# A four-layer graph network on one core: first group's products plain and by halves, layer 1's gamma and beta folded into its weights, and the last values of layer 3 moved to the end

## The chip, the cores and the metric

The kernel runs on one core of a Trainium2 chip. The time is the device time of one execution in microseconds, taken as the median of the runs. The profile shows one execution, with the engines PE (TensorE matmul), PEld (TensorE's weight loads, which overlap PE), DVE (VectorE), ACT (ScalarE), POOL (GpSimd) and SP (SyncE, which here issues transfers).

## The reference

128 graphs of 64 nodes with 512 features go through four layers. Each layer normalizes, applies a relu, and adds the output of an attention over the graph's adjacency. All data are 32-bit floats. 128 graphs x 64 nodes are 8192 rows.

```python
# layers 0 and 2 (4 heads of 64), adjacency as mask
h = relu(layernorm(x))
q, k, v = h @ Wq, h @ Wk, h @ Wv                    # 512 -> 256
x = x + softmax(mask(q k^T / 8)) v @ Wo + bo        # 256 -> 512

# layer 1 (8 heads of 64), adjacency | eye as mask
h = relu(layernorm(x))
h = layernorm(h) * gamma + beta                     # a second one, inside the layer
q, k, v = split(h @ w_qkv.T)                        # 512 -> 3 x 512
x = x + softmax(mask(q k^T / 8)) v @ w_out.T + b_out

# layer 3 (8 heads of 64)
h = relu(layernorm(x))
m = h @ map_w.T + map_b
n = m / max(norm of each head, 1e-8)
cos_adj = (n n^T > 0.1)                             # and not masked
q, k = m @ q_w.T + q_b, m @ k_w.T + k_b
p = softmax(mask(q k^T / 8)) * keep
adj = cos_adj * p
sem = h @ gcn_map_w.T + gcn_map_b
x = x + relu((adj @ sem @ gcn_W.T) / (adj.sum(-1) + 1))
```

## The kernel before

The rows go through in 16 groups of 512 (`NG = 16`, each four blocks of 128). The program is written as a set of streams; each yields the engine it wants and a rough duration, and an ordering loop (`Order`) fixes, when the program is built, in which order each engine gets its instructions. On the chip each engine then runs its list in order and waits where data are not there yet. A smaller `prio` wins among streams that could start at the same moment.

A projection of 512 x 512 is done by Winograd's form of Strassen's method: seven products of halves rather than eight, with four sums of weight quarters (`sums_of_a`) and four sums of input quarters (`sums_of_b`) made beforehand, mostly on POOL.

```python
r_qk = ring("qk", 3, [P, NC, TB * P])       # q, k of a group
r_t  = bank("t", 3, [P, NC, 2, H])          # sums of the input quarters
r_v  = bank("v", 2, [P, TB, 8 * (N + 1)])
r_e  = ring("e", 2, [P, 16, N])             # softmax of half a group
r_pt = ring("pt", 1, [P, 2, 4, P])
r_sc = ring("sc", 1, [P, 2, 512], space=ps) # scores and values in PSUM

def product(bank, A, B, tokens_out, first):          # four calls of 128x256
    for m in range(2):
        for k in range(KC):                          # KC = 2 here
            nc.tensor.matmul(...)

def weights():
    for key, parts in units:         # qk0, vo0, q1, k1, v1, o1, qk2, ...
        ...                          # DMA of the parts, from ACT's queue
        w_ready[key].set()
        yield from sums_of_a(o_part(t) if key in ("vo0", "vo2") else t)
        w_sums[key].set()

def scaled_chunks(s, h):             # layer 1 only
    for half in range(2):
        yield n_ready[1, s, half]
    for c in range(NC):
        ...                          # four transposes into pt
        nc.scalar.activation(h[:, c, :], pt..., AF.Identity,
                             bias=beta[:, c:c + 1], scale=gamma[:, c:c + 1])

def transposes(steps):
    for l, s in steps:
        ...
        if l == 1:
            yield from scaled_chunks(s, h)
        for half in range(2 if l != 1 else 0):
            yield n_ready[l, s, half]
            ...                      # four transposes and one copy a block
            nc.scalar.copy(h[:, :, b * P:(b + 1) * P], pt)
        T, t_done[l, s] = yield from r_t.new("T")
        h_ready[l, s].set()
        yield from sums_of_b(quarters(h), T)

class Out:
    def first(self, i, k, p_, read, done):           # the eviction of a product
        if self.bias is None:
            nc.scalar.copy(o, p3)
        else:
            for m in range(2):
                nc.scalar.activation(o[:, m], p3[:, m], AF.Identity, bias=...)
```

In layer 3 a group's projections are `map`, then `sem`, `q`, `k`; in the last group `q`, `k`, `sem`. The values of `sem` get a row added on POOL (`add_rows`, four instructions), and `p_ready` waits for that. A group's softmax comes in two halves (`front`), each followed by the cosine mask, and `last` transposes each half and multiplies it by the values.

```python
order = ("q", "k", "sem") if end else ("sem", "q", "k")
...
def front(l, s):
    for u, blocks in enumerate(units):               # two halves in layer 3
        S, se = yield from scores(z["q"], z["k"], 2 * nch, blocks)
        E, e = yield from softmax_parts(S, se, m, ...)   # E from r_e
        ...
        C, ce = yield from scores(z["n"], z["n"], 4, blocks)
        ...                                          # Cf = C > 0.1, E *= Cf

def last(s):
    for u in range(2):
        yield z["e_ready", u]
        pt, pte = yield from transposed(*z["e", u])
        for b, t in enumerate(blocks):
            po, poe = yield from r_sc.new("po3")
            ...                                      # 32 small products
            od.spawn(finish(s, t, po, poe, got), 0)
```

Of the kernel before, what the change touches and what calls it, by code (L numbers as in the profile page):

```python
# [8 lines left out]
F32 = mybir.dt.float32  # L9
# [194 lines left out]
def gnn_stack(ctx: ExitStack, tc: tile.TileContext, a: dict, out: bass.AP):  # L204
# [65 lines left out]
    vecs = const.tile([P, 6, NC], F32, name="vecs")  # L270
    nc.scalar.dma_start(vecs, a["vecs"].rearrange("p (v c) -> p v c", c=NC))
    gamma, beta, map_b, q_b, k_b, gcn_b = (vecs[:, i, :] for i in range(6))
    gcn_row = const.tile([P, D], F32, name="gcn_row")


# [13 lines left out]
    def o_part(t):  # L289

        return t.rearrange("p a k n -> p (a k) n")[:, 4:11, None, :]
# [24 lines left out]
    def sums_of_b(B, T, vector=False):  # L316

        n = T.shape[2]
        for o, i0, i1 in ((T[:, 0], B(0, 1), B(0, 0)), (T[:, 1], B(1, 1), T[:, 0]),
# [4 lines left out]
            else:  # L324
                yield pool(0.65 * n)
                nc.gpsimd.tensor_tensor(o, i0, i1, ALU.subtract)  # L326

    def weights():
        for key, parts in units:
            if key == "q1":  # L330
                yield p_ready[0, 0]
            t, w_done[key] = yield from r_w.new(f"w_{key}")
            W[key] = t
            for src, dst in parts(t):
                yield ("actq", 1.0, 10.0)
                nc.scalar.dma_start(dst, src.rearrange("(c p) o -> p c o", p=P))
            if key in ("vo0", "o1", "vo2"):
                l = int(key[-1])
                src = a[f"bo{l}"]
                bo[l], bo_done[l] = yield from r_u.new(f"bo{l}")  # L340
                yield ("actq", 0.5, 2.0)
                nc.scalar.dma_start(bo[l], bass.AP(tensor=src.tensor, offset=src.offset,
                                                   ap=[[0, P], [1, D]]))
            if key == "sem3":
                yield from gcn_fold(t)
            w_ready[key].set()
            yield from sums_of_a(o_part(t) if key in ("vo0", "vo2") else t)
            w_sums[key].set()

    def quarter(t, c, i):  # L350

        return t[:, 2 * i + c // 2, c % 2, :]

    def gcn_fold(t):

# [51 lines left out]
                                 scale=rs[:, 0, t:t + 1])  # L407

    hT, hB, h_ready, h_done, t_done = {}, {}, {}, {}, {}

    def quarters(v):

# [29 lines left out]
                normed[l, s, half] = x, xe  # L442
                n_ready[l, s, half].set()

    def scaled_chunks(s, h):

        for half in range(2):
            yield n_ready[1, s, half]
        x = [normed.pop((1, s, half)) for half in range(2)]
        for c in range(NC):  # L450
            pt, pe_ = yield from r_tr.new("ptr")
            for b in range(TB):
                yield pe(0.115)
                nc.tensor.transpose(pt[:, b, :], x[b // 2][0][:, b % 2, c * P:(c + 1) * P], ident)  # L454
            if c == NC - 1:
                for _, xe in x:
                    xe.set()
            yield act(0.6)
            nc.scalar.activation(h[:, c, :], pt.rearrange("p b k -> p (b k)"), AF.Identity,  # L459
                                 bias=beta[:, c:c + 1], scale=gamma[:, c:c + 1])  # L460
            pe_.set()

    def transposes(steps):

        for l, s in steps:
            h, h_done[l, s] = yield from r_h.new("hT")
            hT[l, s] = h
            if l == 1:
                yield from scaled_chunks(s, h)
            for half in range(2 if l != 1 else 0):  # L470
                yield n_ready[l, s, half]
                x, xe = normed.pop((l, s, half))
                for t in range(2):
                    pt, pe_ = yield from r_tr.new("ptr")
                    for c in range(NC):
                        yield pe(0.115)
                        nc.tensor.transpose(pt[:, c, :], x[:, t, c * P:(c + 1) * P], ident)  # L477
                    if t == 1:
                        xe.set()
                    yield act(0.6)  # L480
                    b = 2 * half + t
                    nc.scalar.copy(h[:, :, b * P:(b + 1) * P], pt)  # L482
                    pe_.set()
            if (l, s) == (3, 1):
                yield x_done[2, NG - 1]
            T, t_done[l, s] = yield from r_t.new("T")
            sums = od.event()
            hB[l, s] = (quarters(h), T, sums)
            h_ready[l, s].set()
            yield from sums_of_b(quarters(h), T)  # L490
            sums.set()
# [67 lines left out]
    def winograd(A, BT, tokens_out, out_, used, begun):  # L559
# [46 lines left out]
        od.spawn(out_.alone(1, 0, p_, pe_), 0)  # L606
        od.spawn(when([c11, c12, c22, pe_], used), 0)

    class Heads(Out):


# [50 lines left out]

    st, p_ready, s_ready, p_used, with_ones = {}, {}, {}, {}, []

    def projections(steps):
        for l, s in steps:
            yield h_ready[l, s]
            h, BT = hT[l, s], hB[l, s]
            z = st[l, s] = {}
            end = s == NG - 1  # L670
            if l in (0, 2):
                yield w_ready[f"qk{l}"]
                qk, z["qk_done"] = yield from r_qk.new("qk")
                used = yield from unit(W[f"qk{l}"], (*BT, w_sums[f"qk{l}"]), False, Out(quarters(qk)))
                od.spawn(when([used], s_ready[l, s], t_done[l, s],
                              w_done[f"qk{l}"] if end else None), 0)
                z["q"], z["k"] = qk[:, 0:2, :], qk[:, 2:4, :]
                yield w_ready[f"vo{l}"]
# [7 lines left out]
                od.spawn(when(es, p_ready[l, s], h_done[l, s]), 0)  # L686
            elif l == 1:
                es = []
                for n in "qk":
                    yield w_ready[f"{n}1"]  # L690
                    o, z[f"{n}_done"] = yield from r_qk.new(f"{n}T")
                    es.append((yield from unit(W[f"{n}1"], (*BT, w_sums[f"{n}1"]), False,
                                               Out(quarters(o)))))
                    od.spawn(when([es[-1]], w_done[f"{n}1"] if end else None), 0)
                    z[n] = o
                od.spawn(when(es[:2], s_ready[l, s]), 0)
# [9 lines left out]
            else:  # L706
# [4 lines left out]
                m_sums, z["n_ready"], m_used = od.event(), od.event(), od.event()  # L711
                od.spawn(sums_after(m_ready, mv, z, m_sums), 1)
                od.spawn(norms(mT, s, m_ready, z["n_ready"], m_used), 3)
                order = ("q", "k", "sem") if end else ("sem", "q", "k")
                es, rows = [], od.event()
                for n in order:
                    yield w_ready[f"{n}3"]
                    if n == "sem":
                        V, z["v_done"] = yield from r_v.new("S2")
                        S2 = V.rearrange("p t (h e) -> p t h e", e=N + 1)  # L720
                        if not any(V is v for v in with_ones):

                            with_ones.append(V)
                            yield pool(0.6)
                            nc.gpsimd.memset(S2[:, :, :, N:N + 1], 1.0)

                        def sv(i, k, S2=S2):
                            return S2[:, 2 * k:2 * k + 2, 4 * i:4 * i + 4, 0:N]
                        used = yield from unit(W["sem3"], (*BT, w_sums["sem3"]), True, Heads(sv))
                        od.spawn(when([m_ready, used], t_done[l, s], h_done[l, s]), 0)  # L730
                        od.spawn(add_rows(S2, used, rows), 0)
                        z["v"] = S2
                        continue
                    yield m_sums
                    o, z[f"{n}_done"] = yield from r_qk.new(f"{n}T3")
                    es.append((yield from unit(
                        W[f"{n}3"], (mv, z["T"], w_sums[f"{n}3"]), False,
                        Out(quarters(o), q_b if n == "q" else k_b))))
                    z[n] = o
                    if n == "k":  # L740
                        z["n"] = mT
                        od.spawn(when(es, s_ready[l, s], m_used, z["T_done"]), 0)
                od.spawn(when(es + [rows], p_ready[l, s]), 0)

    def sums_after(e, B, z, done):
        yield e
# [78 lines left out]
                                             lT[r, c, k], rT[r, c, k], start=True, stop=True)  # L825
        return S, e

    def softmax_parts(S, se, mask, neg):

        m = mask.rearrange("p b k -> p (b k)")  # L830
        n = m.shape[1]
# [6 lines left out]
        mx = small.tile([P, 16], F32, tag="mx", name="mx")  # L838
        yield dve(1.2)
        nc.vector.tensor_reduce(mx, S3, AX.X, ALU.max)  # L840
        E, e = yield from r_e.new("E")
        yield dve(1.2)
        nc.vector.tensor_tensor(E, S3, mx[:, :, None].to_broadcast([P, 16, N]), ALU.subtract)  # L843
        se.set()
# [6 lines left out]
        nc.vector.reciprocal(sm, sm)  # L851
        yield pool(1.95)
        nc.gpsimd.tensor_mul(E, E, sm[:, :, None].to_broadcast([P, 16, N]))  # L853
        return E, e

    def transposed(E, e):

# [197 lines left out]
    def front(l, s):  # L1055
# [6 lines left out]
            z["e_ready", u] = od.event()  # L1062
        p_used[l, s].set()
        for u, blocks in enumerate(units):
            S, se = yield from scores(z["q"], z["k"], 2 * nch, blocks)
            if u == len(units) - 1:
                for n in ("q", "k", "qk"):
                    if f"{n}_done" in z:
                        z[f"{n}_done"].set()
            m = mask[:, blocks[0]:blocks[0] + len(blocks)]  # L1070
            E, e = yield from softmax_parts(S, se, m, (0, 1, 0, 2)[l])
            if u == len(units) - 1:
                me.set()
            z["e", u] = E, e
# [22 lines left out]
    def last(s):  # L1097
# [3 lines left out]
        for u in range(2):  # L1101
            blocks = [2 * u, 2 * u + 1]
            yield z["e_ready", u]
            pt, pte = yield from transposed(*z["e", u])
            for b, t in enumerate(blocks):

                po, poe = yield from r_sc.new("po3")
# [24 lines left out]
    def attentions(steps):  # L1132
        for l, s in steps:
            yield p_used[l, s]
            yield p_ready[l, s]
            yield from (attention(l, s) if l < 3 else last(s))


# [61 lines left out]
```

## Time and profile before

| | |
|---|---|
| time, median of 3 runs | 2985.18 us (2980.7 to 2989.06) |
| span of the profiled execution | 2978.9 us |
| POOL's sums of a weight quarter, 128x512 | 1.3 us each |
| matmul calls of a projection by seven products | 28, of 128x256 each |
| ACT, eviction with scale and bias in layer 1's transposes, x64 | 783 ns |
| ACT, eviction of transposes by a copy, x192 | 592 ns |
| ACT, eviction of q in layer 1 by copies, from mA, x48 | 585 ns |
| ACT, eviction of q in layer 3 with a bias, from mA, x96 | 470 ns |

The profile gives the busy time of each engine; a busy PE is a PE with a matmul in flight, which is not a PE at its peak. A row of the timeline has the start in us, the duration in us, the engine, the line of the kernel, the operation, what is written from what, the shapes and the count; in square brackets stands the idle time before it and what ended it. A full-precision matmul leaves two records, so a count of records is twice a count of calls; a transpose leaves one.

### The profile page before, as it was taken

To read this page: it belongs to the slowest core of one execution; us is meant where nothing else is said; L and a number is where in the kernel's file an instruction comes from. 1 tells how busy PE (TensorE), PEld (TensorE's weight loads), DVE (VectorE), ACT (ScalarE), POOL (GpSimd) and SP (SyncE) were. 2 spreads that over 40 slices of the span, in tenths; PEclk is the share of its full clock that TensorE was granted. 3 is DMA by queue.
4 is the path that set the end of the run, shared out by engine and by line. 5 is a ranking of instruction groups with operands and counts; after the bars stand their busy time and mean duration, and the time that the engine had idled before them with its cause. 6 is when DMAs were issued, how large, how long until landed. Compare 5 with 4: busy or idle time off the path is not lost.

```text
span 2978.9 us, 63888 instructions
## 1 busy us (share of the span) xinstructions
PE 2910.6 (98%) x27176; PEld 2468.1 (83%) x27176; DVE 1727.3 (58%) x2748; ACT 1336.6 (45%) x2361; POOL 1465.2 (49%) x1144
## 2 busy tenths in 40 slices
PE   8999999999999999999999999999999999999997
PEld 6888888888888888888888888887888787888876
DVE  5665566664554555445456556556666666665566
ACT  4444445544444444433444444454444444444442
POOL 6666667444344334335566566663344343344332
PEclk9999999999999999999999999999999999999998
DMA  5323333211112112113233332422232222222212
GB/s 163 116 88 123 95 101 126 67 62 66 48 45 73 59 44 73 59 44 98 94 114 104 102 116 88 138 82 64 72 90 83 63 62 66 70 85 71 52 48 62
DMA packets 162957, 244.05 MB, mean 82 GB/s; under 512 B 17392, under 2 KB 69616, under 8 KB 162672
## 3 DMA queue, kind: packets, MB, share of 16 engines
q1 hardware_dynamic: 149760, 226.56, 24.3%
q10 hardware_dynamic: 12912, 13.42, 1.4%
q8 instruction: 213, 3.49, 0.5%
q14 instruction: 72, 0.59, 0.1%
HBM read 168.60 MB, written 71.30 MB: 81 GB/s over the span
## 4 chain that ended last, share of the span: by engine, by line
PE 85%; DVE 6%; ACT 4%; DMA 2%; POOL 2%; issue 1%; SPq 0%; DVEq 0%; ACTq 0%; POOLq 0%
PE mA L516 37%; PE mC L516 18%; PE mB L516 10%; PE sc L824 4%; PE mmv L659 4%; PE ptp L864 3%; PE ptr L477 3%; PE po L983 2%; ACT E L846 1%; PE po L1118 1%; DVE E L843 1%; DVE sc L835 1%; DVE mx L840 1%; PE mmn L773 1%; PE ptr L454 1%
## 5 line engine op out<-in xcount | busy, mean ns | idle before, releaser
L853 POOL TENSOR_TENSOR E<-E,sm 128x1024 f32<-128x1024 f32 x96 | 186.3, 1941 | 424.2 <-DVE sm L851 298.7
L390 DVE BATCH_NORM_STATS2 st<-xin 128x6 f32<-128x512 f32 x320 | 215.6, 674 | 260.2 <-DMA xin<-x 206.9
L929 POOL TENSOR_TENSOR xres<-xres,u 128x512 f32<-128x512 f32 x192 | 243.4, 1268 | 250.0 <-ACT u L924 245.0
L908 POOL TENSOR_TENSOR xres<-xres,u 128x512 f32<-128x512 f32 x192 | 257.7, 1365 | 219.5 <-DMA xres<-x 99.6
L406 ACT ACTIVATE xin<-xin,rs 128x512 f32<-128x512 f32 x320 | 243.7, 808 | 110.9 <-DVE rs L399 110.7
L397 POOL TENSOR_TENSOR rs<-rs,mhalf 128x2 f32<-128x2 f32 x160 | 118.4, 740 | 276.9 <-DVE rs L395 270.3
L659 PE MATMUL mmv<-w_vo,hT 128*128 128x256 f32 x1024 | 233.4, 380 | 0.9 <-DVE xres L542 0.9
L659 PEld LDWEIGHTS mmv<-w_vo,hT 128*128 128x128 f32 x1024 | 193.5, 190 | 29.0 <-DVE xres L542 2.6
L326 POOL TENSOR_TENSOR t<-hT 128x512 f32<-128x512 f32 x128 | 178.3, 1393 | 73.2 <-ACT hT L482 39.0
L326 POOL TENSOR_TENSOR t<-hT,t 128x512 f32<-128x512 f32 x128 | 172.3, 1346 | 50.5 <-ACT hT L459 46.6
L399 DVE SCALAR_TENSOR_TENSOR rs<-mv,rs 128x2 f32<-128x2 f32 x160 | 80.3, 502 | 197.7 <-POOL rs L397 197.7
L516 PE MATMUL mA<-t,w_qk 128*128 128x256 f32 x768 | 187.0, 380 | 2.8 <-ACT qk L529 2.5
L516 PE MATMUL mA<-t,w_k 128*128 128x256 f32 x768 | 182.7, 381 | 4.8 <-ACT kT L533 4.7
L516 PE MATMUL mA<-t,w_q 128*128 128x256 f32 x768 | 187.1, 379 | 0.0
L516 PEld LDWEIGHTS mA<-t,w_k 128*128 128x128 f32 x768 | 144.8, 190 | 28.2 <-ACT kT L533 8.3
L516 PEld LDWEIGHTS mA<-t,w_qk 128*128 128x128 f32 x768 | 143.1, 190 | 22.0 <-ACT qk L529 3.3
L868 ACT COPY pt<-ptp 128x512 f32<-128x512 f32 x192 | 112.7, 588 | 105.1 <-PE ptp L864 105.1
L516 PEld LDWEIGHTS mA<-t,w_q 128*128 128x128 f32 x768 | 143.1, 190 | 18.1
L849 DVE TENSOR_REDUCE sm<-E 128x16 f32<-128x1024 f32 x96 | 116.4, 1212 | 69.5 <-ACT E L846 69.5
L757 POOL TENSOR_TENSOR v<-v,gcn_row 128x512 f32<-128x512 f32 x64 | 81.4, 1305 | 150.4 <-ACT v L615 150.4
L482 ACT COPY hT<-ptr 128x512 f32<-128x512 f32 x192 | 113.7, 592 | 74.1 <-PE ptr L477 74.1
L846 ACT ACTIVATE E<-E 128x1024 f32<-128x1024 f32 x96 | 101.5, 1058 | 83.6 <-DVE E L843 83.3
(210 smaller groups left out, 6819.0 us busy)
## 6 DMA issues: line engine op xcount, KB each, us to landing
x<-xres SPq DMA_DIRECT2D x96, 512.0 KB, 3.8
xin<-x SPq DMA_DIRECT2D x96, 512.0 KB, 3.8
xres<-x SPq DMA_DIRECT2D x64, 512.0 KB, 4.2
xin<-in_x SPq DMA_DIRECT2D x32, 512.0 KB, 3.8
xres<-in_x SPq DMA_DIRECT2D x32, 512.0 KB, 4.6
u<-rs SPq DMA_DIRECT2D x128, 128.0 KB, 3.1
xres<-x SPq DMA_DIRECT2D x256, 64.0 KB, 2.3
out<-xres SPq DMA_DIRECT2D x256, 64.0 KB, 2.1
```

The lines of the kernel that those rows point to most:

```text
L326: nc.gpsimd.tensor_tensor(o, i0, i1, ALU.subtract)
L390: nc.vector.bn_stats(st, v[:, t, :])
L397: nc.gpsimd.tensor_tensor(rs[:, 0, :], rs[:, 1, :], mhalf[:, :2], ALU.pow)
L406: nc.scalar.activation(v[:, t, :], v[:, t, :], func, bias=rs[:, 2, t:t + 1], scale=rs[:, 0, t:t + 1])
L516: nc.tensor.matmul(o, l, r, start=(first and m == 0 and k == 0), stop=(k == KC - 1), skip_group_check=True)
L659: nc.tensor.matmul(p_[:, 0:n], inT[:, c, t * P:(t + 1) * P], w[:, c, :], start=(c == 0), stop=(c == NC - 1))
L824: nc.tensor.matmul(S[a_ * N:(a_ + 1) * N, par, col], lT[r, c, k], rT[r, c, k], start=True, stop=True)
L846: nc.scalar.activation(E, E, AF.Exp, scale=0.125)
L849: nc.vector.tensor_reduce(sm, E, AX.X, ALU.add)
L853: nc.gpsimd.tensor_mul(E, E, sm[:, :, None].to_broadcast([P, 16, N]))
L908: nc.gpsimd.tensor_add(xr[:, t, :], xr[:, t, :], bo[l])
L929: nc.gpsimd.tensor_add(v, v, both(u))
```

## The change

It has three parts.

- **First group.** The first projection of layer 0 is done for group 0 by eight plain products rather than seven with sums, so that it needs no sums and can begin when half of the group's transposed input is there. The sums of that weight are made after it, for the other groups.
- **Layer 1.** Gamma is multiplied into the rows of the weights for q, k and v, on POOL. Beta times the weights becomes a bias: for q and k it is added when the products are evicted, for v it goes through the output projection into the bias that is added to the residual. The transposes of layer 1 are then like those of the other layers, a half at a time, and their evictions are plain copies.
- **The end of layer 3.** The last two groups leave their `sem` projections until after q and k of the last group, so that products are left for PE while the last softmaxes run. The last half of the last softmax takes a buffer from the ring of q and k rather than from the ring of two for softmaxes. `last` waits for the values only after it has transposed.

```diff
@@ weights
-            yield from sums_of_a(o_part(t) if key in ("vo0", "vo2") else t)
-            w_sums[key].set()
+            if key in ("q1", "k1", "v1"):
+                yield from gamma_into(key)
+            elif key == "o1":
+                yield from v_bias()
+            ...
+            if key == "qk0":
+                od.spawn(sums(key, t, plain_done), 4)
+            else:
+                yield from sums(key, o_part(t) if key in ("vo0", "vo2") else t)
+
+    def gamma_into(key):
+        i = ("q1", "k1", "v1").index(key)
+        t, e = yield from r_mm.new("mmb")
+        for oc in range(NC):
+            for c in range(NC):
+                yield pe(0.15)
+                nc.tensor.matmul(t[:, oc:oc + 1], quarter(W[key], c, oc // 2)[
+                    :, (oc % 2) * P:(oc % 2 + 1) * P], beta[:, c:c + 1], start=(c == 0), stop=(c == NC - 1))
+        yield dve(0.2)
+        nc.vector.tensor_copy(bv if i == 2 else qkb[:, i, :], t[:, 0:NC])
+        e.set()
+        for c in range(NC):
+            for i in range(2):
+                yield pool(0.7)
+                v = quarter(W[key], c, i)
+                nc.gpsimd.tensor_scalar_mul(v, v, gamma[:, c:c + 1])
+
+    def v_bias():
+        ...
+        for c in range(NC):
+            for i in range(2):
+                yield pe(0.43)
+                nc.tensor.matmul(t[:, i * H:(i + 1) * H], bb[:, c, :], quarter(W["o1"], c, i),
+                                 start=(c == 0 and i == 0), stop=(c == NC - 1),
+                                 skip_group_check=True)
+        yield dve(0.7)
+        nc.vector.tensor_add(bo[1], bo[1], t)
@@ transposes
-            if l == 1:
-                yield from scaled_chunks(s, h)
-            for half in range(2 if l != 1 else 0):
+            for half in range(2):
...
+                if (l, s, half) == (0, 0, 0):
+                    hT[l, s] = h
+                    h_half.set()
+            if (l, s) == (0, 0):
+                hB[l, s] = quarters(h), None
+                h_ready[l, s].set()
+                continue
@@ new
+    def plain(A, h, out_, used):
+        B = quarters(h)
+        es = []
+        for k in range(2):
+            if k:
+                yield h_ready[0, 0]
+            for i in range(2):
+                p_, e = yield from (r_ma if i else r_mm).new("mP")
+                yield from product(p_, A[:, 2 * i], B(0, k), False, True)
+                yield from product(p_, A[:, 2 * i + 1], B(1, k), False, False)
+                od.spawn(out_.alone(i, k, p_, e), 0)
+                es.append(e)
+        od.spawn(when(es, used), 0)
@@ projections, layer 1
-                                               Out(quarters(o)))))
+                                               Out(quarters(o), qkb[:, i, :]))))
@@ projections, layer 3
-                order = ("q", "k", "sem") if end else ("sem", "q", "k")
+                late = s >= NG - 2
+                if late:
+                    behind.append((s, z, BT, m_ready, rows))
+                for n in ("q", "k") if late else ("sem", "q", "k"):
...
+                if end:
+                    for b in behind:
+                        yield from sem(*b)
@@ front
+            if (l, s, u) == (3, NG - 1, 1):
+                E, e = yield from r_qk.new("E")
+                ...
+            else:
+                E, e = yield from r_e.new("E")
@@ last
             pt, pte = yield from transposed(*z["e", u])
+            yield p_ready[3, s]
```

## The prediction

> **What bounds the kernel now.** I read the page first, for the busy shares.
>
> ```profile
> PE 2910.6 (98%) x27176; PEld 2468.1 (83%) x27176; DVE 1727.3 (58%) x2748; ACT 1336.6 (45%) x2361; POOL 1465.2 (49%) x1144
> ```
>
> TensorE is busy for 2910.6 of 2978.9 us, so at most 68 us of its idle time can be won, and an instruction added to it is paid nearly in full. Next the table of stretches, to see where the 68 us lie (columns: stretch, its length, then busy time and count for PE, PEld, DVE, ACT, POOL, then the granted clock).
>
> ```profile
> 0.00:40.00 40.00, 27.14 (x181) 23.14 (x182) 18.26 (x51) 17.88 (x28) 23.45 (x27) 1.00 0.59 182
> ...
> 2940.00:2960.00 20.00, 14.20 (x211) 11.50 (x209) 15.46 (x17) 6.74 (x13) 8.56 (x6) 0.94 0.12 32
> 2960.00:2979.00 19.00, 7.71 (x173) 6.42 (x168) 9.73 (x18) 1.17 (x2) 1.75 (x1) 0.50 0.25 57
> ```
>
> 12.9 us are idle in the first 40, 17.1 in the last 39; layer 1 (600 to 1440 us) has none at all. So the ends are where an order can win, and layer 1 is where nothing can. Then the timeline of the start:
>
> ```profile
> 12.73 3.96 POOL L314 TENSOR_TENSOR w_qk<-w_qk 128x512 f32<-128x512 f32 x3 [1.36 <-DMA w_qk<-in_Wk]
> 14.80 3.62 PE L516 MATMUL mA<-hT,w_qk 128*128 128x256 f32 x8
> 16.64 1.27 POOL L326 TENSOR_TENSOR t<-hT 128x512 f32<-128x512 f32 x1
> 21.87 1.03 PE L516 MATMUL mC<-t,w_qk 128*128 128x256 f32 x4
> 24.69 0.66 PE L477 MATMUL ptr<-ident,xin 128*128 128x128 f32 x4 [1.79 <-ACT xin L406]
> ```
>
> The first product begins at 14.80, once all of hT is there, and PE then stands still before 24.69, because group 1's layernorm queues on POOL behind the sums. Last, PE's timeline of the end:
>
> ```profile
> 2951.15 1.16 PE L824 MATMUL sc<-kT,qT 64*64 64x64 f32 x64 [0.29 <-DVE Cf L1085]
> 2952.48 1.10 PE L864 MATMUL ptp<-ident,E 128*128 128x128 f32 x8 [0.17 <-DVE E L1091]
> 2958.74 1.37 PE L1118 MATMUL po<-v,pt 64*64 64x65 f32 x32 [5.16 <-ACT pt L868]
> 2961.45 1.99 PE L824 MATMUL sc<-m 64*64 64x64 f32 x64 [1.34 <-DVE y L1034]
> 2964.87 1.15 PE L1118 MATMUL po<-v,pt 64*64 64x65 f32 x32 [1.43 <-DVE Cf L1085]
> 2966.11 1.97 PE L864 MATMUL ptp<-ident,E 128*128 128x128 f32 x8
> 2971.02 1.15 PE L1118 MATMUL po<-v,pt 64*64 64x65 f32 x32 [1.34 <-DVE y L1034]
> ```
>
> After about 2951 no products of projections are left; the last softmax runs alone, its scores at 2951.15 and its transposes only at 2966.11.
>
> **Unit costs, all from this trace.** A full-precision product call leaves two records; eight records of 128x256 stand 1.73 us apart in the timeline of layer 1, so one record takes 0.216 us and a call 0.43. One Winograd product is four calls, 1.73 us; a projection is seven of them, 12.1 us. A small product of 128x128x128 is known from the fold of layer 3:
>
> ```profile
> 1488.90 1.95 PE L363 MATMUL mmf<-bdw,raw 128*128 128x128 f32 x16
> ```
>
> that is 0.122 us a record.
>
> **What the Trainium skill says.** "TensorE: Matmul & The Clock Gate", section on the HAM clock gate: the array runs at half clock until some 3.4 us of sustained work, and again after as much idleness. The trace agrees: the eight records at 14.80 took 3.62 us against 1.73 later, and the eight transposes at 2966.11 took 1.97 where four take 0.44 in the chain of waits. The same page, section LDWEIGHTS: a weight load takes columns / 1.2 ns, 107 ns for 128, whatever the moving side is. The 0.122 us above is compatible; no run so far has a one-column product. "ScalarE: Activation LUTs", What ACT_TABLE_LOAD costs: about 1283 ns; the groups show 32 loads of 1283 ns in layer 3 (Sqrt against Exp) and one at the start. The section on table sets has Identity in every set, so a biased eviction adds no load.
>
> **The change part by part.**
>
> *First group plain.* It takes eight products for seven: +1.73 us. It needs half of hT, ready when the second ACT copy ends, 11.69 + 0.59 = 12.3 us, and Wq and Wk (landed by 12.7); i = 0 needs only Wq. So PE starts about 2.2 us earlier. No sum of hT or W is on its way, and POOL is free for group 1's layernorm: the 1.8 us before 24.69 go. The half-clock loss stays: 3.62 - 1.73 = 1.9 us in either. A check by totals: by 40.74 before had done 88 records of 0.216, 32 transposes of 0.109 and one set of scores of 1.09, 23.6 us of work. With 0.9 done before 12.3, the new one does the other 22.7 plus 1.7 plus 1.9, so reaches that state at 38.6 if nothing stops it: 2 us won. That is all, although 12.9 us look idle. w_vo is also issued right behind w_qk, rather than at 18.46; PE was not waiting for it.
>
> *Gamma and beta into the weights.* Removed: the scale and bias in 64 evictions of transposes (783 ns, becoming copies of about 592); on ACT only. Transposes stay as many. Added on PE: 16 one-column calls for each of q, k, v: 48 calls, 96 records, each with a 128-column weight load. Estimate from the skill's LDWEIGHTS rate: 96 x 0.107 = 10.3 us; the trace's 0.122 for the next larger shape gives 11.7 as a ceiling. I take 10. v_bias: eight calls of 128x256, 3.45 us. Added on POOL: 24 multiplies of 128x256; POOL's sums of that shape for w_vo took 3.48 us for four, so at most 0.87 each, 21 us. Two thirds of it (q and k) falls into 50 to 110 us, where POOL is at 31.5 of 40 us; it has low priority, and I give PE 1 us of stalls for it.
>
> *Biased evictions of q and k in layer 1.* Four of each projection become two activations of 470 ns (rows of L533, 0.84 us a pair in the timeline) in place of one copy of 585: +0.26 us x 4 x 2 x 16 = 33 us of ACT, less 64 x 0.19 = 12 in the transposes. ACT is at 26 of 60 us there. Each eviction is hidden behind another product of 1.73 us if it comes promptly. What it may cost is in layer 3's rows of PE's waits (total us, times, longest):
>
> ```profile
> PE mC L516 <- ACT m L533: 8.6, 15, 0.6
> ...
> PE mA L516 <- ACT kT L533: 4.7, 4, 1.2
> ```
>
> The first row is a table load in front of the eviction; layer 1 has none. q in layer 3 waits nowhere. I give 1.5 us.
>
> *The tail.* Two sem projections, 24.2 us, move behind k of group 15, and the softmax of its second half gets its own buffer. From that group's first scores (2936.97) to the transposes of the second half (2966.11) the softmaxes took 29 us; with 24.2 us of sem products and about 7 of scores, transposes and values beside them they can hide. What remains after the last sem product: evictions 0.9, four row additions on POOL at about 1.3 each 5.2, then four rounds of values at half clock, 1.2 each with 1.3 of DVE between, and the transposes of the last half, 2.5: some 16 us, of which 3.4 is work at full clock. So 12.6 us are lost, where before lost 14.3 idle between 2820 and 2972 and 3.5 to the half clock. The end after the last value, 6.7 us, stays. Gain 17.8 - 12.6 = 5; less 2 for new stalls, as map of group 14 is no longer followed by its sem: 3 us.
>
> Sum: +1.7 - 4.0 (start) + 10 + 3.45 + 1 (POOL) + 1.5 (evictions) - 3 (tail) = +10.6. I shade it to +7, as one-column loads may be pulled ahead better than estimated.
>
> **Rivals.** *The ends win more than the fold costs.* For it: 30 us idle at the two ends. Against it: the start's idle is mostly the wait for x, and the end's is a serial chain that keeps its last links. If one-column records take 0.05 us and the tail gives 8, the sum is 2978. *Layer 1's evictions become the bound.* For it: the 0.57 us per group of the first row above. Against it: ACT idles 2.9 us before many of the evictions there. If both q and k wait 0.57 in all 16 groups, 18 us more: 3008. *POOL saturates in layer 0.* 21 us more work while it paces the layernorms and sums; if two thirds of it hit PE, 3005. *Hidden anyway:* a changed order might put the fold's products into PE's waits at the passage between layers 0 and 1 (3.2 us idle in 480 to 540); 2988.
>
> **Range and chances.** The error is the one-column term (5), the tail (4), the start (2), evictions and POOL (4), the spread of runs (3): about 8 in all. So 2992 us, 2981 to 3003; 2% is 60 us, more than any part reaches. Faster by over 2% 0.005, within 2% 0.985, slower by over 2% 0.01.
>
> **What would show it.** The first product of w_qk at about 12.4 us, and group 1's first w_qk product near 38.6 (40.74 before). 96 one-column records at about 0.11 us: nearer 0.03 would break the sign. PE's busy time up by some 12 to 15 us. Layer 1's stretches still full, with waits on qT and kT under 2 us in sum. Between the last sem product and the end some 22 us, with POOL's row additions first. I am wrong if the fold's records come cheap, if the tail shrinks by over 8 us, or if waits on L533 appear in every group.

## The result, and the profile after

The changed kernel takes 3016.0 us (median of four runs, 3013.62 to 3018.47) against 2985.06 (2980.7 to 2989.06): ratio 1.0104, 95% interval 1.0087 to 1.0122. It is about 31 us slower. The prediction had +7 and a range up to 3003: the direction holds, the time lies outside the range.

The page's first part, of the changed kernel:

```profile
PE 2938.8 (97%) x27296; PEld 2492.8 (83%) x27296; DVE 1731.9 (57%) x2750; ACT 1358.1 (45%) x2488; POOL 1489.9 (49%) x1164
```

TensorE has 120 records more: 96 one-column ones, 16 for the bias of v, 8 for the eighth product. Its busy time grew by 28.2 us, and the prediction expected 12 to 15. The span of the profiled execution grew by 37.8, so idle time grew as well, by some 10. (The profiled execution before was the shortest of its runs and the one after the longest of its; the medians differ by 31.)

The table of stretches shows where both lie (columns: stretch, length, then busy time and count for PE, PEld, DVE, ACT, POOL, then granted clock, DMA share, GB/s):

```profile
0.00:40.00 40.00, 27.41 (x185) 23.11 (x186) 15.53 (x49) 15.89 (x25) 13.84 (x21) 1.00 0.55 180
60.00:120.00 60.00, 57.83 (x439) 49.35 (x439) 33.08 (x58) 23.80 (x40) 45.94 (x41) 0.89 0.24 82
...
480.00:540.00 60.00, 57.28 (x493) 48.78 (x483) 34.30 (x63) 27.22 (x48) 43.48 (x39) 0.94 0.34 107
...
3000.00:3016.00 16.00, 2.29 (x64) 1.97 (x64) 4.33 (x10) 0.00 (x0) 0.00 (x0) 0.50 0.45 101
```

Two of these stretches in the kernel before:

```profile
60.00:120.00 60.00, 57.64 (x461) 49.15 (x461) 40.59 (x61) 28.63 (x50) 46.92 (x37) 1.00 0.40 126
480.00:540.00 60.00, 56.79 (x450) 48.16 (x449) 40.83 (x68) 29.94 (x49) 43.53 (x36) 1.00 0.31 102
```

Three things are new. The first 40 us are no fuller than before: 12.6 us idle, 12.9 before. In 60 to 120 and 480 to 540 the granted clock is 0.89 and 0.94, though PE is busy for 57 to 58 of 60 us; before it was 1.00 in both. And in the last 16 us PE does 2.29 us of work.

The start, in the timeline of the changed kernel (start, duration, engine, line, operation; idle time before it in brackets):

```profile
5.73 2.30 ACTq L343 DMA_DIRECT2D w_vo<-in_Wo  x2
...
8.81 1.28 ACT L457 ACT_TABLE_LOAD   x1 [8.81 <-DVE rs L450]
...
13.62 5.91 PE L556 MATMUL mP<-hT,w_qk 128*128 128x256 f32 x16 [0.68 <-ACT hT L514]
15.69 3.01 POOL L315 TENSOR_TENSOR w_vo<-w_vo 128x256 f32<-128x256 f32 x4 [7.26 <-DMA w_vo<-in_Wo]
18.67 0.71 POOL L448 TENSOR_TENSOR rs<-rs,mhalf 128x2 f32<-128x2 f32 x1
```

The same power in the kernel before:

```profile
10.68 0.69 POOL L397 TENSOR_TENSOR rs<-rs,mhalf 128x2 f32<-128x2 f32 x1 [2.09 <-DVE rs L395]
```

The first product begins at 13.62, not at 12.4. The transfers of w_vo, now issued right behind w_qk, hold up ACT's list: its table load comes at 8.81, before at 5.94, and its first normalization at 10.11, before at 8.82. Worse, the sums of w_vo stand in POOL's list ahead of the power that the second half's layernorm needs. POOL waits 7.26 us for w_vo, makes the sums, and gets to that power at 18.67; before it was done at 10.68. PE runs out of transposed halves and waits 0.94 us for the next. Group 1's first product with w_qk starts at 41.72; before at 40.74; predicted 38.6.

The one-column products, in PE's timeline (three stretches of it):

```profile
56.10 4.14 PE L376 MATMUL mmb<-vecs,w_q 128*128 128x1 f32 x32
60.10 2.05 PE L556 MATMUL mC<-hT,w_qk 128*128 128x256 f32 x4
61.95 3.62 PE L556 MATMUL mA<-t,w_qk 128*128 128x256 f32 x8
...
96.66 1.62 PE L376 MATMUL mmb<-vecs,w_k 128*128 128x1 f32 x14
...
99.30 3.39 PE L376 MATMUL mmb<-vecs,w_k 128*128 128x1 f32 x18
...
521.14 4.88 PE L376 MATMUL mmb<-vecs,w_v 128*128 128x1 f32 x32
525.88 7.50 PE L714 MATMUL mmv<-w_vo,hT 128*128 128x256 f32 x24
```

The 32 records for q take 4.00 us from their start to the next start, 0.125 each. Then the eight product records at 61.95 take 3.41 us from start to start, 3.62 with the pipeline's end, where eight take 1.73 and 1.89 at full clock: the burst has left the array at half clock. The 16 records of products between 60.10 and 66.48 took 6.38 us instead of 3.46, 2.9 too long. The burst for k is split by a set of scores: 14 records in 1.55 us, then 18 in 3.25, and 12 product records after it are 2.2 us too long. After v's (4.74 us), 24 product records take 7.33 instead of 5.18. Together 13.5 us in the bursts and 7.3 behind them: 20.8.

The clock around the three bursts, same columns as above:

```profile
56.00:59.00 3.00, 3.00 (x29) 2.97 (x27) 3.00 (x3) 0.00 (x0) 3.00 (x3) 1.00 0.03 5
59.00:66.00 7.00, 7.00 (x21) 5.83 (x21) 4.54 (x12) 1.86 (x3) 5.28 (x7) 0.51 0.00 1
...
100.00:107.00 7.00, 7.00 (x25) 6.16 (x25) 4.14 (x5) 2.98 (x4) 3.51 (x4) 0.51 0.01 2
...
523.00:530.20 7.20, 7.20 (x27) 6.37 (x28) 3.08 (x8) 1.89 (x3) 7.20 (x8) 0.53 0.73 230
```

PE counts as busy for all of it, 7.00 of 7.00, and still the clock is at half for 6.8 us of each of these stretches. It falls before the bursts are over, 2.9 us into q's and 2.1 into v's. Three times 6.8 us at half clock lose 10.2 us. Before the clock falls a one-column record takes 0.111 us (14 of them in 1.55). So the 20.8 us are about the 10.3 that the prediction had for 96 records at full clock, and 10.2 of half clock.

The end, in the timeline of the changed kernel (SPq is the list of SyncE, which issues the transfers):

```profile
2994.57 5.71 SPq L1090 DMA_DIRECT2D xres<-x  x8
...
2998.58 0.69 DVE L1111 SCALAR_TENSOR_TENSOR xres<-y,xres 128x512 f32<-128x512 f32 x1 [4.44 <-DMA xres<-x]
...
3000.46 1.15 PE L1196 MATMUL po<-v,pt 64*64 64x65 f32 x32 [3.13 <-DVE y L1105]
...
3003.06 1.15 PE L1196 MATMUL po<-v,pt 64*64 64x65 f32 x32 [1.45 <-DVE y L1105]
...
3011.04 0.69 DVE L1111 SCALAR_TENSOR_TENSOR xres<-y,xres 128x512 f32<-128x512 f32 x1 [3.27 <-DMA xres<-x]
```

The last softmax is hidden as meant. But DVE waits 4.44 us for the residual, which SyncE asks for only at 2994.57, and with DVE the next values of PE wait. After the last value's products, at 3004.2, it takes 12.5 us to the end; before it took 6.7. The waits of the last 47 us put a number on it (total us, times, longest):

```profile
DVE xres L1111 <- DMA xres<-x: 8.6, 3, 4.4
...
DVE xres L1111 <- DMA out<-xres: 3.1, 1, 3.1
```

The residuals of the last group go into two buffers that hold group 14's output until it is stored. Its values have moved to the end too, so its stores come last, and 16 loads and 32 stores, each some 0.6 us on SyncE's one list, alternate from 2979 to 3014.

### The profile page after: what moved, and what is told of

It reads as the page before. It is cut to its first block, busy times and chain, and to the rows that moved or that the text cites. A ratio compares the mean times of both kernels' runs of the same rounds, so it can differ in the third digit from the quotient of the medians.

```text
span 3016.7 us, 64289 instructions
## 1 busy us (share of the span) xinstructions
PE 2938.8 (97%) x27296; PEld 2492.8 (83%) x27296; DVE 1731.9 (57%) x2750; ACT 1358.1 (45%) x2488; POOL 1489.9 (49%) x1164
## 4 chain that ended last, share of the span: by engine, by line
PE 84%; ACT 4%; DVE 4%; POOL 3%; DMA 2%; issue 1%; SPq 1%; DVEq 0%; POOLq 0%; ACTq 0%
PE mA L556 36%; PE mC L556 18%; PE mB L556 9%; PE mmv L714 5%; PE sc L897 4%; PE ptr L509 4%; PE ptp L935 3%; PE po L1054 2%; ACT E L918 1%; PE po L1196 1%; DVE sc L908 1%; DVE E L915 1%; PE mmn L846 1%; POOL t L327 1%; DVE mx L913 1%
## 5 line engine op out<-in xcount | busy, mean ns | idle before, releaser
L450 DVE SCALAR_TENSOR_TENSOR rs<-mv,rs 128x2 f32<-128x2 f32 x160 | 72.1, 451 | 207.3 <-POOL rs L448 207.2
L514 ACT COPY hT<-ptr 128x512 f32<-128x512 f32 x256 | 151.8, 593 | 77.9 <-PE ptr L509 77.9
L509 PE MATMUL ptr<-ident,xin 128*128 128x128 f32 x1024 | 159.1, 278 | 11.9 <-ACT xin L457 11.9
```

## The experiments

**The yardstick.** The kernel before ran beside each of these on the same chip, with medians of 2983.14, 2981.44 and 2981.51 us on the three chips used. So I compare ratios to it, and give us as (ratio - 1) x 2985. The expectations name absolute times; a difference of 3 us to them can be the chip's. The change itself stands at 1.0104, +31.0 us. An interval of four runs is about +-4.5 us, so a difference between two such kernels is uncertain by some 7 us: effects of 3 to 4 us are not resolved by the times. Every kernel below keeps one small edit of the change: a softmax takes its buffer before its scores and not after. In the last kernel (the new tail alone) it shows no cost: the time is that of before, and layer 1 begins at 508.96 against 507.91.

**Theory and rivals.** Theory: the parts add up, and each went wrong in its own way (half clock after the bursts; w_vo ahead of the layernorm; residual loads behind stores). Rivals: the bursts cost only their own records; any one-column product drops the clock, however few; the tail lost to its values' half clock and not to its transfers.

**Each part undone.** First layer 1 as before, gamma and beta in the evictions of the transposes again, the other two parts kept:

```diff
-            if key in ("q1", "k1", "v1"):
-                yield from gamma_into(key)
-            elif key == "o1":
-                yield from v_bias()
+            # transposes of layer 1: scaled_chunks, as before
```

> The changed kernel with layer 1's gamma and beta applied at the transposes again, as before; the other two parts stay. Theory 'the fold': each of the three bursts of 32 one-column records takes 4.0 to 4.8 us and leaves 2 to 3.5 us of half clock behind it, 20.8 us in all, and the bias of v 3.7; part of this was made up by fewer stalls at the start of layer 1 (about 4). So 3016 - 20 = 2994 to 2997, and layer 1 begins near 509 us rather than 533. Rival 'the order': any reshuffle of the lists costs some 25 us in layer 0 through other waits; then layer 1 still begins after 525 and the time stays above 3008.

Measured 2999.09 us, ratio 1.0049 (1.0034 to 1.0063): it takes 16.4 of the 31 us away. Layer 1's first product starts at 512.50; after at 533.21, before at 507.91. So 20.7 us of the fold are spent before layer 1 begins, close to the 20.8 of the bursts and what follows them.

Then layer 3 in the old order, with the old buffers:

```diff
-for n in ("q", "k") if late else ("sem", "q", "k"):
+for n in ("q", "k", "sem") if end else ("sem", "q", "k"):
```

> The changed kernel with layer 3's projections in the old order and the last softmax in its old buffer; the other two parts stay. Theory 'the tail loses': between the map of group 13 and the end the change lost 7.6 us, as stores of group 14 and residual loads of group 15 now share SyncE's list at the very end; so 3008. Rival 'the tail wins its 3 us as predicted and the loss is elsewhere': 3019.

Measured 3005.99, 1.0073 (1.0056 to 1.0089): 9.3 us less. The new tail loses, though by how much the times leave wide open; the trace has 7.3 (below).

Then the first group by seven products with sums:

```diff
-            if (l, s) == (0, 0):
-                hB[l, s] = quarters(h), None
-            ...                       # eight plain products
+            # group 0 like the others
```

> The changed kernel with the first group by seven products again; the other two parts stay. Theory 'the start is a wash': before had the first group's values projected at 40.7 us, the changed kernel at 41.9, because POOL's list has the sums of w_vo ahead of the second half's layernorm; so 3015, with the values done near 40.7. Rival 'plain wins 2 us as predicted, and something else in the first 60 us is slow': 3018 to 3020.

Measured 3010.86, 1.0092 (1.0077 to 1.0107): 3.6 us less, an interval that overlaps the change's. Group 1's first w_qk product is at 42.38 here, so the start alone is no better without the plain products; layer 1's first product is at 530.35, 2.9 earlier than after. The clock alone can make up those 2.9 us: around q's and v's bursts it was at half for 3.4 us in this execution and not 6.8, which is 3.4 us less lost. So the times do not show what the plain products cost. The three undos sum to 29.3 of 31.0, which agrees with parts that add.

**Bias products 128 columns wide.** The same 96 records, with beta copied into 128 columns as the moving side, and column 0 of each result taken:

```diff
-nc.tensor.matmul(t[:, oc:oc + 1], w, beta[:, c:c + 1], ...)
+nc.vector.tensor_copy(bw, beta[:, :, None].to_broadcast([P, NC, P]))   # once for each weight
+nc.tensor.matmul(t[:, oc * P:(oc + 1) * P], w, bw[:, c, :], ...)
```

> The changed kernel, but the bias products take beta copied 128 wide as their moving side (the same 96 records with the same weights, 128 columns in place of one). Theory 'idle array': the array counts as idle while one-column products stream, which drops the clock to half; with 128 columns the records take about the same 0.125 us each, the clock stays full, and the 8.6 us of half clock behind and in the three bursts go: 3007, with no records of 0.46 us a pair behind the bursts. Rival 'the clock falls for another reason (a wait at that place)': half clock stays after the bursts, 3016. Rival 'columns cost': 128 columns make the records longer, over 0.2 us each, 3022.

Measured 3007.38, 1.0079 (1.0064 to 1.0095): 7.5 us less. PE's timeline of this kernel, and then its table of stretches, over the burst and over layers 0 and 1:

```profile
62.73 3.84 PE L380 MATMUL mmb<-bw,w_q 128*128 128x128 f32 x32
...
67.70 1.89 PE L720 MATMUL mmv<-w_vo,hT 128*128 128x256 f32 x8
```

```profile
62.00:64.00 2.00, 2.00 (x67) 1.93 (x59) 1.38 (x5) 0.61 (x1) 0.81 (x1) 1.00 0.00 0
...
54.00:1480.00 1426.00, 1414.89 (x12591) 1225.15 (x12590) 809.94 (x1293) 661.05 (x1159) 738.82 (x583) 1.00 0.24 78
```

The burst takes 3.67 us for 128 times the arithmetic, and the eight product records at 67.70 take 1.89 with the pipeline's end, the full rate. The clock never leaves 1.00 from 54 to 1480, so it falls behind none of the three bursts, and layer 1's first product comes at 521.35, 11.9 us before the change's. The other runs agree: the mean granted clock is 0.994 to 0.995 in all four, 0.990 to 0.993 in the change's four. So the one-column bursts cost twice: once for their records, which a wide moving side hardly makes dearer, and once for the half clock that comes with them. The rival that they cost only their records falls.

**The same records in bursts of eight.** If the clock falls after some us of nearly empty array, short bursts should not drop it:

```diff
-        t, e = yield from r_mm.new("mmb")
         for oc in range(NC):
+            t, e = yield from r_mm.new("mmb")
             for c in range(NC): ...
+            nc.vector.tensor_copy(dst[:, oc:oc + 1], t[:, oc:oc + 1])
+            yield ("pause", 3.0, 0.0)
```

> The changed kernel with the same 96 one-column records, but in bursts of 8 with other products of some 3 us between. Theory 'idle array': what counts is how much of a few microseconds the array streams; no half clock follows, so the 8.6 us go as in the run with wide columns: 3007. Rival 'any one-column product drops the clock': twelve drops in place of three, over 3020.

Measured 3022.0, 1.0135 (1.012 to 1.0151): slower than the change by 9 us, where I expected a gain. PE's timeline shows both halves of it, and the table of stretches the clock:

```profile
56.24 0.95 PE L376 MATMUL mmb<-vecs,w_q 128*128 128x1 f32 x8
57.05 1.11 PE L557 MATMUL mC<-hT,w_qk 128*128 128x256 f32 x4
...
138.90 1.98 PE L898 MATMUL sc<-qk 64*64 64x64 f32 x64 [0.72 <-ACT qk L570]
```

```profile
60.00:120.00 60.00, 53.65 (x450) 44.90 (x448) 31.93 (x58) 24.44 (x44) 40.60 (x34) 1.00 0.27 90
```

Eight records in 0.81 us leave the clock alone here: four records of products behind them take 1.11, and 60 to 120, with the other three bursts of q, has 1.00. So "any one-column product drops the clock" falls. But behind a burst of k, with waits of 0.97 and 0.72 us near it, the scores take 1.98 instead of 1.16: a short burst next to idle time still came before a fall. And twelve bursts that each take a buffer put waits on PE which the change had not: PE is busy for 53.65 us in 60 to 120, 57.83 after, with single waits of 1.76 (transposes for the values), 1.70 (residual) and, later, 2.85 (a bias product for v's eviction). This was the fastest of the four runs, 3017.65 us with a mean clock of 0.994; the other three have 0.991, as low as the change. So whether short bursts spare the clock as a rule, and what the 9 us are made of, stays open.

**w_vo asked for later**, behind the first half of group 0's transposed input:

```diff
+            if key == "vo0":
+                yield h_half
```

> The changed kernel, but w_vo is asked for only when half of the first group's transposed input is there. Theory 'the early weights are in the way': ACT's five transfer issues delayed its first normalization by 1.3 us, and POOL's list had the sums of w_vo, which waited for its landing at 15.7, ahead of the second half's layernorm at 18.7; without both, PE works from 12.3 us without a gap and has the first group's values done near 38.6 us rather than 41.7: 3013. Rival 'the start doesn't matter': later waits in layer 0 take it back, 3016.

Measured 3009.46, 1.0093 (1.0078 to 1.0108): 3.3 us less, within what the interval leaves open. The trace is plainer: first product at 12.11 (predicted for the change 12.4), group 1's first at 39.82 (41.72 after). That the order of w_vo spoils the start is shown; that mending it brings the whole 1.9 us to the end is not. Layer 1's first product comes 6.7 us earlier, at 526.48, but 3.4 of that is clock again: around k's and v's bursts it was at half for 3.4 us and not 6.8.

**The plain first group alone**, in the kernel before, with w_vo later:

> The kernel before with the plain first group alone, w_vo asked for later; layer 1 and layer 3 as before. By my sum for the start (2.2 us earlier, 1.8 us of waiting gone, 1.7 for the eighth product) 2981; by adding the single effects measured so far (3016 - 17 - 10 - 3) 2986, that is, no gain.

Measured 2984.03 in 20 runs, 1.0010 (1.0004 to 1.0017): not faster, a little slower than before. (The change less the effects of fold, tail and w_vo's order is 1.0007.) Group 1's first product comes at 39.10, 1.6 us ahead of before, where 2.1 was predicted; layer 1's comes at 509.4 against 507.91. The gain is had, and given back: from 40 us to layer 1 PE waits 11.2 us, before 7.9 (this is one execution, the slowest of the 20). One place shows how. The timeline, first of this kernel, then of before, sums for the second projection:

```profile
49.99 1.12 DVE L324 TENSOR_TENSOR t<-m 128x256 f32<-128x256 f32 x1 [1.83 <-ACT m L1081]
...
52.44 1.48 DVE L324 TENSOR_TENSOR t<-m 128x256 f32<-128x256 f32 x1
```

```profile
49.62 0.43 DVE L323 TENSOR_TENSOR t<-m 128x256 f32<-128x256 f32 x1 [0.99 <-ACT m L992]
...
50.67 2.70 POOL L908 TENSOR_TENSOR xres<-xres,u 128x512 f32<-128x512 f32 x2 [1.27 <-DMA xres<-in_x]
50.75 1.49 DVE L323 TENSOR_TENSOR t<-m,t 128x256 f32<-128x256 f32 x1
```

The same sum takes 0.43 us or 1.48. In the first kernel POOL makes its own two-input sums from 49.56 to 57.69 nearly without a break. In the kernel before POOL is idle until 50.67, while the first three of the four sums begin; the fourth begins behind POOL's sum and takes 1.49. The Trainium skill, "GPSIMD Engine Reference", Specifications, says that its SBUF interfaces are shared with VectorE, with contention where a DVE instruction has two inputs in SBUF; the 0.43 against 1.48 and 1.49 agree. How much of the 3.3 us of waits comes from it was not measured by a run of its own.

**Residuals of the last group earlier**, into buffers of the input that are free by then:

```diff
-v2, e2 = yield from r_xres.new()
+v2, e2 = yield from (r_xin if s == NG - 1 else r_xres).new()
...
+for r in ([s, s + 1] if s == NG - 2 else ...):
+    od.spawn(last_residuals(r, ahead[r]), 2)
```

> The changed kernel, but the residual rows of the last group are loaded when group 14's values begin, into buffers of the layernorm's input ring, which is idle by then; in the changed kernel they wait for the two residual buffers that group 14's stores hold. Theory 'the queue': at the end SyncE's list alternates 16 loads and 32 stores at 0.6 us each, and the last values wait for residuals (8.6 us of waits on DVE); with the loads out of the way the end follows the last value by 6.7 us rather than 12.5, and the four waits for y fall to 1.3 us: 3008. Rival 'the chain': row additions on POOL and the serial rounds of values set the end anyway: 3014.

Measured 3002.28, 1.0072 (1.0057 to 1.0087): 9.6 us less, more than expected. SyncE's list in this kernel:

```profile
2904.80 11.74 SPq L1090 DMA_DIRECT2D xin<-x  x16
...
2970.99 13.24 SPq L1118 DMA_DIRECT2D out<-xres  x16
2986.07 11.01 SPq L1118 DMA_DIRECT2D out<-xin  x16
```

The loads are issued some 70 us before they are needed, and only stores are left. From the first product of group 15's map to the end it takes 103.0 us, 112.3 in the change: 9.3 less. Values of group 15 in PE's timeline:

```profile
2983.09 0.70 PE L1200 MATMUL po<-v,pt 64*64 64x65 f32 x32 [1.08 <-DVE Cf L1162]
2985.46 0.77 PE L1200 MATMUL po<-v,pt 64*64 64x65 f32 x32 [1.67 <-DVE y L1105]
...
2991.08 1.15 PE L1200 MATMUL po<-v,pt 64*64 64x65 f32 x32 [1.35 <-DVE y L1105]
```

The last values are at half clock as in the change, but two of the four rounds are not (0.70 and 0.77 us for 32, against 1.22 and 1.15), and with the scores and transposes near them that makes up to some 2 of the 9.3 us, by an estimate from the lengths of these groups in the two traces. The 5.3 us behind the last value's products (7.2 to the end, 12.5 in the change) have no products in them, so there it was the late loads. The run moves the loads to other buffers and earlier in the list at once; which of the two held them more was not separated.

**Put together.** Without the fold, with w_vo later and residuals early (the other two parts kept and mended):

> The changed kernel with layer 1 as before, w_vo asked for later, and the last group's residuals loaded early. By adding the single effects: 2999 - 3 - 8 = 2988, so within 5 us of the kernel before. If the tail then really wins the 3 us of the prediction and the start 2, it is 2979. If the effects don't add, above 2993.

Measured 2983.62, 1.0009 (1.0000 to 1.0018). The single effects add to 1.0006 (1.0104 less 0.0055, 0.0011 and 0.0032): without the fold and with the two mends the loss is gone, as their sum has it.

All three parts kept, all mended (wide bias products, w_vo later, residuals early):

> The change with all three of its faults mended: bias products 128 columns wide, w_vo asked for later, residuals of the last group loaded early. By adding the single effects (-8.6, -6.5, -13.7) from 3016: 2987. What is left above the kernel before would be the fold's own records, 12 us, and the bias of v, 3.7, less what start, tail and layer 1's beginning win. If the effects overlap, 2993 or more.

Measured 2997.2, 1.0052 (1.0036 to 1.0067). Single effects add to 1.0036, the edge of the interval, so chance, an overlap of the mends or a new wait can be the rest; the trace has two waits in layer 0 that the change had not, 2.5 us for an eviction of qk and 2.3 for the copy of beta to 128 columns.

The new tail alone in the kernel before, with residuals early:

> The kernel before with the late sem projections and the last softmax's own buffer alone, and the last group's residuals loaded early; first group and layer 1 as before. Theory 'the tail wins once the queue is clear': 3 to 5 us under the kernel before, 2979 to 2981, ratio 0.998 to 0.999. Rival 'it is break-even, the gain seen was order luck elsewhere': 2984 to 2986.

Measured 2980.11 in 13 runs, 0.9998 (0.9990 to 1.0006): the same as before. No version beat the kernel before by what these runs can tell.

## Why the prediction was wrong, by its own steps

**The bound.** Right: PE is nearly full, and what was added to it was paid. The rival in which the ends win more than the fold costs has not come.

**96 x 0.107, taken as 10 us.** This is the step of the fold that failed: 20.8 us, twice the term. The rate itself was about right, 0.111 us a record at full clock. What the term left out is the half clock that the bursts bring, 3 x 6.8 us, in part within them and in part behind. I took the time of a weight load for the whole cost. The prediction had quoted the Trainium skill, "TensorE: Matmul & The Clock Gate", Part 1 on the HAM clock gate, that about 3.4 us of idleness bring the half clock, and had counted it only at the two ends. I took a PE with matmuls in flight for a busy one. In the change the clock fell 2.9 and 2.1 us after a burst of 32 had begun; one burst of 0.81 us did not do it, nor did 3.67 us with 128 columns. So the gate counts something other than the busy time of the profile, and the moving columns are what differs.

**v_bias, 3.45.** Right: eight calls, 566.46 to 570.18, 3.7 us.

**POOL 1 and evictions 1.5.** The evictions cost nothing: no PE wait at all shows in layer 1, and the 4.1 us of PE waits which before had at that layer's start (1.9 for v, 1.6 for qT, 0.6 for pt) are gone too. So the fold nets 20.8 + 3.7 - 4.1 = 20.4 us in the trace, 16.4 by the undo, against 16 predicted. That the sum came near was luck: errors ran against each other, a term half its size, a gain not seen and 2.5 us of stalls that did not come.

**The start, +1.7 - 4.0.** Failed. "w_vo is also issued right behind w_qk ... PE was not waiting for it" was the sentence that hid it: PE doesn't wait for w_vo, but ACT's and POOL's lists do. Group 1's first product came 1.0 us later than before and not 2.1 earlier. With w_vo later the working is confirmed to half a us (12.11, and 39.1 where the eight products stand alone), although its loss to the half clock, 1.9 us, set 3.62 us with the pipeline's end against 1.73 without; from start to start it is 3.41, so 1.7. But then a second thing fails: time won by 40 us is not time won at the end, since it turned into waits before layer 1. With layer 1's work as before, layer 1 still starts 4.6 us later than before (512.5). What the start costs at the end, 3.6 us by the undo, is not resolved by the times.

**The tail, -3.** Failed, and it is the largest error of the three parts: +9.3 by the undo, 7.3 by the trace. The sem products hide the softmax as worked out, the row additions take 5.50 us (5.2 predicted), and the loss to map of group 14 without its sem is 3.2 us of PE waits (2 predicted). Between the last sem product and the end 33 us pass, where the prediction had some 22. "The end after the last value, 6.7 us, stays" is the line that failed: 12.5. From the first product of group 15's map, before took 96.1 us and would have taken 108.2 with the 12.1 us of a sem projection added; after took 112.3, so +4.1 where the working had -5; with the 3.2 of group 14 that is 7.3. I never asked what group 14's late stores would do to the loads that share their buffers and their list. With that mended it takes 103.0, the -5 of the working.

**The sum.** Predicted -2.3 + 16 - 3 = 10.6; by the three undos 3.6 + 16.4 + 9.3 = 29.3. So start and tail carry the miss, 6 and 12 us; inside the fold the errors are, by the trace, 10.8 - 4.1 - 2.5. The shading to +7 went the wrong way.

**Not settled.** In the profiled pair, one wait at the passage to layer 3 (products for the fold there, waiting for a residual) was 4.7 us before and 7.2 after; it lies between 4.8 and 7.1 in the eleven other kernels, and I found no rule. Some 3 us of the pair's 37.8 have no place.

## What to carry to other kernels

Ask of an operation added to a full TensorE not only what it takes but what it leaves: matmuls of one moving column, 4 us of them in a row, brought the half clock here and with it cost twice their own records (20.8 us for 10.3); make the moving side wide, or put them where the clock is low anyway (not tried here). When values or stores move to the end of a kernel, list the transfers that share their buffers and their queue, and issue loads whose data is long there before the stores fill it. And a wait that PE doesn't have can still sit in the list of ACT or POOL in front of what PE needs next.

## What the hardware showed that I had not expected

- At full clock one-column full-precision records take 0.10 to 0.11 us (8 in 0.81, 14 in 1.55), 128-column ones 0.115 (32 in 3.67): the narrow product is hardly cheaper.
- 32 one-column records in a row brought the clock from 1.00 to 0.50 with PE busy throughout. In the traces of the five kernels with three such bursts it stayed there for 6.8 us at nine of the fifteen and for 3.4 us at six.
- A wait of PE of some 2 us without a one-column product near it came before a half clock of 3.4 us too (1.93 us before 62.20 with the fold undone, 1.97 before 571.05 with short bursts).
- A DVE sum of 128x256 takes 0.42 us, and 1.1 to 1.5 while POOL makes two-input sums.
- SyncE issues a transfer each 0.6 us or so: 48 in the tail fill about 35 us, more than the work of any engine there.
